# Two row points at a time in a convolution by polynomial points: interpolation in pairs, the infinite row by columns in two images, copies placed behind evictions

## The chip, the cores and the metric

The kernel runs on one core of one Trainium2 chip. The metric is the device time in microseconds of one execution; the time of a kernel is the median over several runs. TensorE multiplies matrices, VectorE does elementwise work between tiles, ScalarE does copies and activations, GpSimd (POOL) fills and loads, and SyncE (SP) issues most DMA transfers. In the profile these are PE, DVE, ACT, POOL and SP; PEld is the loading of weights into TensorE, which overlaps its matmuls.

## The reference, cut to what matters

The input x is 4 images of 256 channels, 64 by 64, in float32. Layer 0 makes 49 attention weights for each pixel and applies them to 49 shifted copies of the image; layer 1 whitens the result.

```
k = conv(x, w1, 7x7, dilation 2, padding 6) + b1        # 256 -> 128 channels
k = conv(k, w2, 1x1) + b2                               # 128 -> 49 channels
attn = softmax(k, axis=1)
y = sum over (u, v) of attn[:, 7u+v] * shift(x, 2u-6, 2v-6)
# layer 1, per group of 64 channels over all images and pixels:
Sigma = eps*I + cov(y);  five Newton steps P -> Sigma^(-1/2)
out = (P @ (y - mean(y))) * weight + bias
```

Nothing stands between the two convolutions, so the kernel folds w1 and w2 into one 7 by 7 convolution to 49 channels.

## The kernel before, in words

**Convolution by points.** A convolution with dilation 2 falls apart into four ordinary 7 by 7 convolutions, one for each parity of row and column. The kernel computes them as products of polynomials: along the rows and along the columns, input and filter are evaluated at seven points, numbered 0 to 6 in the code (the values 0, 1, -1, 2, -2, 1/2, and INF, the leading coefficient), multiplied, and interpolated. `row_eval` (L422) evaluates the input along the rows at one row point into the buffers `rb`, by VectorE. `col_eval` (L454) evaluates this along the columns, bank by bank, into the tiles `xh`. Column points go in three banks, `BANKS` = ((1, 2, 0), (3, 4, 6), (5,)), where 6 is INF. `weights` (L354) does the same for the filter; a row point's weights are computed once, stored in DRAM (`gd`), and loaded into `wr` by SP for each later image. There is one buffer for each `xh` and one `wr` for each bank, so the next row's operands can be made once the bank that reads them has been multiplied.

`conv_bank` (L483) multiplies one bank: a full row point takes 208 TensorE instructions over its three banks, in the kept order, and after each bank one ScalarE copy (L512, with high priority) evicts PSUM into the tile `pv` of the row. `col_interp` (L553) interpolates along the columns through `interpolate` (L517): 22 VectorE operations on 113 partitions, 19 of 162 elements and 3 of 144, and one ScalarE copy (L567) for the fourth output. Its results are row `br` of `zz`. When all row points of an image are there, `row_interp` (L570) does the same along the rows, 17 operations in its part 0 and 5 in its part 1, of 576 and 512 elements, and ScalarE adds the bias into the logits. The elementwise helpers are `add`, `sub` and `madd` (L300, L303, L307).

**The row point INF** does not go through column points. `direct_inf` (L632) loads its filter taps into `wi` and `direct` (L597, matmuls at L608) convolves the fourth row phase of the input along the columns directly: 56 TensorE instructions. The result goes to one of two tiles `zi`, whose last row POOL clears (L586).

**Order of the work.** Image 0 has a prologue in strict order: row points 1, 2 and 3 by columns, INF, 0, 4 and 5 directly (`direct0`), while the filter is being made. Then the loop at L1143 goes over images 1 to 3. In each, the list of steps is INF (cost 12) and for each of the rows 0 to 5 the three banks (costs 6, 5, 2). In image 1 INF comes after row 0, between the two parts of image 0's softmax (`soft`); in images 2 and 3 it is the first step. Each step, `conv_step` (L656), multiplies a bank, then prepares the same bank of the next row (`prepare`, L647), and after the last bank interpolates the columns. For the last two rows of an image this is held in written order (`in_order`) together with the parts of `row_interp`.

After each eighth of the summed costs, `gap` runs a piece of the weighted sum of the image before: transposes of the input (L926) copied to `xb` (L934), matmuls with `band` (L955), transposes of the result (L987) copied to `yt` (L995), and second moments (L1008). The attention weights go through DRAM (`sd`) into `band`, and VectorE transposes them there (L908). Softmax starts from transposed logits (L797) with a maximum on VectorE (L803, L806) and exponentials on ScalarE (L811).

[...] On VectorE and ScalarE a scheduler decides the order when the kernel is built, from dependences and priorities[...]. The last part of the kernel, after the last image's logits, finishes the weighted sum, computes the whitening matrices and writes the output.

Of the kernel before, what the change touches and what calls it, by code (L numbers as in the profile page):

```python
# [23 lines left out]
INF = 6  # L24
# [3 lines left out]
ROWS = (0, 1, 2, 3, 4, 5)  # L28
# [3 lines left out]
def kernel(  # L32
# [222 lines left out]
    zz = apool.tile([P, NP - 1, Q9, W], F32, name="zz")  # L255
    zi = [apool.tile([P, Q9, W], F32, name=f"zi{k}") for k in range(2)]
    for k in range(2):
        nc.gpsimd.memset(zi[k], 0.0)
    ct = apool.tile([P, Q8 * 4 * Q8, 4], F32, name="ct")
    it = ct.rearrange("p a b -> p (a b)")[:, :PT].rearrange("p (q b) -> p q b", q=Q9)  # L260
# [10 lines left out]
    gd = [dram.tile([P, nsl, NSK], F32, name=f"gd{b}") for b in range(NP - 1)]  # L271
# [41 lines left out]
    kept = {br: dram.tile([P, KS * NSK], F32, name=f"g{br}d") for br in (4, 5)}  # L313

# [40 lines left out]
    def weights(b, br, i):  # L355
# [9 lines left out]
        wt = apool.tile([P, ns, NSK], F32, tag=f"wr{i}", name=f"wr_{b}_{br}_{i}")  # L365
# [5 lines left out]
        if br == 0:  # L371
            g = [gr0[:, v] for v in range(KS)]
        elif br in kept:

            f = rb[0].rearrange("p q r c w -> p (q r c w)")[:, : KS * NSK]
            if i == 0:
                nc.sync.dma_start(f, kept[br])
            f = f.rearrange("p (v a r k) -> p v a r k", v=KS, a=NCC, r=2)
            g = [f[:, v] for v in range(KS)]
        else:  # L380
            g = [gbr[:, v] for v in range(KS)]
        g = [t.rearrange("p a r k -> p (a r k)") for t in g]
        e, o, e1 = (
            ct.rearrange("p a b -> p (a b)")[:, k * NSK : (k + 1) * NSK] for k in range(3)
# [38 lines left out]
    def row_eval(b, br, rb=rb):  # L423

        for pr in range(2):
            xs = slots[2 * b + pr].rearrange("p c (q a) w -> p a q c w", a=4)
            r = [t[:, :, pr] for t in rb]
            if br == 1:
                add(r[0], xs[:, 0], xs[:, 2])
                add(r[1], xs[:, 1], xs[:, 3])  # L430
            elif br == 0:
                nc.scalar.copy(r[2], xs[:, 0])
            for cc in range(NCC):
# [18 lines left out]
        return rb[{1: 2, 2: 0, 3: 0, 4: 1, 5: 2, 0: 2}[br]]  # L452
# [27 lines left out]
    pvs = {}  # L480

    def conv_bank(b, br, i, w):

        if i == 0:
            pvs[b, br] = apool.tile(
                [P, NP, Q9, 2 * Q9], F32, tag="pv", name=f"pv_{b}_{br}", bufs=2
            )
# [23 lines left out]
        with tc.high_priority():  # L511
            nc.scalar.copy(  # L512
                pvs[b, br][:K2, i0 : i0 + len(pts)].rearrange("p n q b -> p (n q b)"),
                cv[:K2, : len(pts)].rearrange("p n q b two -> p (n q b two)"),
            )

    def interpolate(pt, tmp, outs, cut, part=None):  # L517
# [9 lines left out]
        if part != 1:  # L527
# [14 lines left out]
            add(tmp, tmp, s4)  # L542
            madd(outs[0], lo(s1), 1.0 / 6, hi(c0))
            add(outs[2], lo(c6), hi(s3))
        if part != 0:
            madd(hh, tmp, -1.0 / 9, hh)
# [3 lines left out]
            madd(outs[1], lo(s4), 1.0 / 15, hi(s2))  # L550

    def phases(t):

        return [t[:, :, bass.ds(4 + a - R if a < R else 0, Q8, 4)] for a in range(4)]

    def col_interp(b, br, part=None):
        pv = pvs[b, br]
        pt = {c: pv[:K2, i] for i, c in enumerate(ORDER)}
        outs = phases(zz[:K2, br].rearrange("p q (w two) -> p q w two", two=2))
        cut = lambda t, k: t[:, :, 2 * k : 2 * (k + Q8)].rearrange("p q (b two) -> p q b two", two=2)  # L560
        t = it
        if part is not None:

            t = pvs[b, ROWS[-2]][:, 0]
        interpolate(pt, t[:K2], outs, cut, part)
        if part != 0:
            nc.scalar.copy(outs[3], cut(pt[5], 0))  # L567

    def row_interp(b, part):

        pt = {k: zz[:K2, k] for k in range(NP - 1)}
        pt[INF] = zi[b % 2][:K2]
# [4 lines left out]
        outs = [t[:, 0] for t in phases(lg[:K2].unsqueeze(1))]  # L577
        cut = lambda t, k: t[:, k : k + Q8]

        tr = zi[(b + 1) % 2]  # L580
        if part == 0:
            interpolate(pt, tr[:K2], outs, cut, 0)
            done_ = ((0, outs[0]), (2, outs[2]))
        else:
            interpolate(pt, tr[:K2], outs, cut, 1)
            nc.gpsimd.memset(tr[:, Q8], 0.0)  # L586
# [7 lines left out]
    def direct(b, br, s, ps, w, xr=None):  # L594
# [22 lines left out]
        z = zi[b % 2][:K2] if br == INF else zz[:K2, br]  # L617
# [7 lines left out]
    gi = dram.tile([P, KS, NCC * KT], F32, name="gi")  # L625
    nc.sync.dma_start(gi, tap[:, UPOS[3]].rearrange("p v a k -> p v (a k)"))

# [3 lines left out]

    def direct_inf(b):  # L632

        t = apool.tile([P, KS, NCC, KT], F32, tag="wi", name=f"wi_{b}")
        nc.sync.dma_start(t.rearrange("p v a k -> p (v a k)"), gi.rearrange("p v k -> p (v k)"))
        w = [t[:, v] for v in range(KS)]
        direct(b, INF, 0, conv_psum(), w)
# [5 lines left out]
    rows += [(b, br) for b in range(1, B) for br in ROWS]  # L643
# [11 lines left out]
    def conv_step(k, i):  # L655
# [14 lines left out]
        if i == len(BANKS) - 1 and not end:  # L670
            if b > 0 and br == ROWS[-2]:
                with in_order():
                    col_interp(b, br)
                    row_interp(b, 0)
            else:
                col_interp(b, br)

# [4 lines left out]
    def direct0(br, sr):  # L682
        if br in kept:
# [36 lines left out]
    nxt.update(weights(0, 3, 0))  # L720
    col_eval(xr, 0)
    direct0(0, 1)
    nxt.update(weights(0, 3, 1))
    col_eval(xr, 1)
    nxt.update(weights(0, 3, 2))
# [3 lines left out]
    col_interp(0, 1)  # L729
    col_eval(xr, 2)  # L730
    bank(2, 0)
    bank(2, 1)
    direct0(4, 0)
    bank(2, 2)
# [12 lines left out]
    col_interp(0, 2)  # L747
    direct0(4, 1)
    col_interp(0, 3)
    row_interp(0, 0)  # L750
    direct0(5, 0)
    for i in three:
        prepare(NR0, i)
    direct0(5, 1)
    row_interp(0, 1)
    strict[0] = False
# [386 lines left out]
    for b in range(1, B):  # L1143

        steps = []
        for r in range(len(ROWS)):
# [237 lines left out]
```

## Time and profile before

| quantity | value |
| --- | --- |
| median of 3 runs | 761.76 us (760.7 to 762.47) |
| the profiled execution | 767.08 us |
| its span in the profile | 765.3 us |
| TensorE busy | 710.7 us (93%) |
| VectorE busy | 630.3 us (82%) |
| ScalarE busy | 332.4 us (43%) |
| POOL busy | 34.4 us (4%) |
| granted TensorE clock, mean | 0.978 |
| convolution by points on TensorE (L502) | 253.7 us in 4368 instructions |
| direct row INF of images 1 to 3, with `wi` (L608) | 34.8 us in 168 instructions |

Durations come from one profiled execution, which took 5.3 us longer than the median of the runs. A line of the timeline gives the start, the busy time, the engine, the line of the code, the operation, output and inputs, the shape, and in brackets how long the engine was idle before and what ended that wait. "128x512 f32" is partitions by elements. A line of busy time by stage gives the stretch of the span, the sum, the busy time of PE, PEld, DVE, ACT and POOL, the granted clock, the DMA share and GB/s.

### The profile page before, as it was taken

What the parts mean: (1) busy time and instruction counts of PE and PEld (TensorE: products, weight loads), DVE (VectorE), ACT (ScalarE), POOL (GpSimd) and SP (SyncE); (2) the same over time, 40 slices, a digit from 0 to 9 for tenths busy, and PEclk for the clock granted to TensorE, in tenths of its full rate; (3) what the DMA queues carried; (4) which work ended last, traced back from release to release, by engine and by line L of the source; (5) the groups of instructions that cost most, each with busy time, mean ns of one, the idle gap of its engine ahead of it and who ended that gap; (6) DMA issues with size and microseconds to landing.
All of it is one profiled execution on the core that took longest, in us unless ns stands there. A gap on an engine that the chain in (4) does not pass through costs nothing.

```text
span 765.3 us, 18542 instructions
## 1 busy us (share of the span) xinstructions
PE 710.7 (93%) x7512; PEld 538.0 (70%) x7512; DVE 630.3 (82%) x1312; ACT 332.4 (43%) x958; POOL 34.4 (4%) x48
## 2 busy tenths in 40 slices
PE   6989899969899999989999999999999889998996
PEld 1449564365798887779988967798898768885322
DVE  3769999999899999989996899699979775645565
ACT  2413241025555454366444443635435473322464
POOL 0410000020000010001000100000000000000000
PEclk9999999979999999999999999999999999999999
DMA  8991110042654393056734920533532233362487
GB/s 323 238 322 65 39 75 38 1 155 68 200 153 156 122 351 91 20 160 205 235 120 141 313 70 1 155 90 110 166 88 80 49 115 128 115 251 111 190 362 327
DMA packets 59773, 114.76 MB, mean 150 GB/s; under 512 B 22903, under 2 KB 42024, under 8 KB 58920
## 3 DMA queue, kind: packets, MB, share of 16 engines
q1 hardware_dynamic: 55992, 94.71, 37.5%
q0 software_dynamic: 3696, 18.88, 7.2%
q8 instruction: 59, 0.97, 0.5%
q14 instruction: 26, 0.21, 0.1%
HBM read 66.23 MB, written 47.33 MB: 148 GB/s over the span
## 4 chain that ended last, share of the span: by engine, by line
DVE 43%; PE 32%; ACT 5%; issue 5%; DMA 2%; SPq 0%; DVEq 0%; ACTq 0%
PE y L955 10%; PE cv L502 7%; DVE xh L307 5%; PE tp L1324 4%; DVE rb L307 3%; DVE pv L307 3%; DVE zz L307 3%; DVE ct L307 3%; DVE ct L300 3%; DVE band L908 3%; PE sig L1008 3%; PE tp L987 2%; PE tp L926 2%; DVE pv L303 2%; DVE rb L300 2%
## 5 line engine op out<-in xcount | busy, mean ns | idle before, releaser
L502 PE MATMUL cv<-xh,wr 128*49 128x128 f32 x4368 | 253.7, 278 | 14.3 <-DVE xh L300 11.5
L502 PEld LDWEIGHTS cv<-xh,wr 128*49 128x49 f32 x4368 | 247.3, 125 | 19.9 <-issue 12.9
L955 PE MATMUL y<-band,xb 128*128 128x224 f32 (+2 forms) x640 | 153.4, 379 | 12.5 <-ACT xb L934 8.3
L955 PEld LDWEIGHTS y<-band,xb 128*128 128x128 f32 x640 | 111.2, 196 | 34.4 <-ACT xb L934 10.8
L974 ACT ACTIVATE slot<-y,pivot 128x512 f32<-128x512 f32 x53 | 36.7, 740 | 60.0 <-PE y L955 60.0
L512 ACT COPY pv<-cv 113x486 f32<-113x486 f32 (+1 forms) x63 | 29.8, 474 | 74.9 <-PE cv L502 73.7
L995 ACT COPY yt<-tp 128x256 f32<-128x256 f32 x128 | 45.5, 379 | 34.8 <-PE tp L987 33.8
L926 PE MATMUL tp<-ident,slot 128*128 128x128 f32 x256 | 50.3, 299 | 7.1 <-ACT yt L995 7.1
L987 PE MATMUL tp<-ident,slot 128*128 128x128 f32 x256 | 52.0, 299 | 4.0 <-ACT xb L934 1.4
L908 DVE STREAM_TRANSPOSE band<-band 128x960 f32<-128x960 f32 (+1 forms) x48 | 50.8, 1059 | 4.9 <-DMA band<-sd 4.8
L987 PEld LDWEIGHTS tp<-ident,slot 128*128 128x128 f32 x256 | 41.3, 205 | 13.9 <-issue 4.5
L926 PEld LDWEIGHTS tp<-ident,slot 128*128 128x128 f32 x256 | 40.0, 206 | 14.4 <-ACT yt L995 9.0
L857 ACT COPY zt<-d 32x112 f32<-32x112 f32 (+2 forms) x156 | 45.0, 288 | 1.7
L811 ACT ACTIVATE d<-tp,mx 128x49 f32<-128x49 f32 x128 | 37.0, 336 | 15.1 <-DVE mx L806 15.1
L307 DVE SCALAR_TENSOR_TENSOR xh<-ct 128x512 f32<-128x512 f32 x42 | 27.7, 681 | 12.2 <-PE cv L502 12.0
L934 ACT COPY xb<-tp 128x256 f32<-128x256 f32 x87 | 30.4, 376 | 15.8 <-PE tp L926 15.2
L1008 PE MATMUL sig<-yt 128*64 128x65 f32 x1024 | 36.9, 225 | 0.0
L1008 PEld LDWEIGHTS sig<-yt 128*64 128x64 f32 x1024 | 32.5, 138 | 6.0 <-issue 4.4
L608 PE MATMUL cv<-slot,wi 128*49 128x496 f32 (+3 forms) x168 | 34.8, 571 | 0.0
L934 DVE COPY xb<-tp 128x256 f32<-128x256 f32 x41 | 16.4, 421 | 22.2 <-PE tp L926 22.2
L307 DVE SCALAR_TENSOR_TENSOR pv<-pv 113x162 f32<-113x162 f32 x105 | 33.5, 319 | 1.0
L419 ACT ACTIVATE wr<-wr 128x392 f32<-128x392 f32 (+1 forms) x36 | 17.3, 512 | 31.1 <-DVE wr L300 18.8
(224 smaller groups left out, 999.9 us busy)
## 6 DMA issues: line engine op xcount, KB each, us to landing
out_dram<-out SPq DMA_DIRECT2D x32, 512.0 KB, 3.4
sd<-zt SPq DMA_DIRECT2D x16, 896.0 KB, 3.9
slot<-in_x_dram POOLq DMA_DIRECT2D x12, 1024.0 KB, 9.6
band<-sd SPq DMA_DIRECT2D x128, 84.0 KB, 2.1
wr<-gd SPq DMA_DIRECT2D x15, 588.0 KB, 3.8
wr<-gd SPq DMA_DIRECT2D x15, 490.0 KB, 3.6
spill<-slot POOLq DMA_DIRECT2D x3, 2048.0 KB, 8.4
back<-spill SPq DMA_DIRECT2D x3, 2048.0 KB, 7.7
```

Source lines behind the costliest of these rows:

```text
L300: return in_turn(TT(o, a, b, ALU.add))
L307: return in_turn(STT(o, a, f, b, ALU.mult, ALU.add))
L502: nc.tensor.matmul(cv[h * HB : h * HB + KT, k, sr : sr + n, sc : sc + n], wv[:, sc, sr, cc], xh[bc][:, :n, h * NCC + cc, :n], start=(j == ...
L811: nc.scalar.activation(d[:, h, i], lt[i // NI][:, i % NI, h, :KT], AF.Exp, bias=mx[:, i, h : h + 1], accum_out=s[:, h, i : i + 1],)
L857: ins = nc.scalar.copy(o, i)
L908: nc.vector.transpose(f, f)
L926: nc.tensor.transpose(t[:, cc * P : (cc + 1) * P], xt[:, cc, CR * m : CR * (m + 1), bass.ds(pc, SW, 2)], ident,)
L934: (nc.vector.tensor_copy if tail else nc.scalar.copy)(xb, t[:, :C])
L955: nc.tensor.matmul(ps[:, cc, q0 - half * HALF : q1 - half * HALF, :], xb[:, cc * P : (cc + 1) * P], rhs, start=(k == 0), stop=(k == len(PI ...
L987: nc.tensor.transpose(t[:, cc * P : (cc + 1) * P], yt[:, cc, CR * i : CR * (i + 1), bass.ds(pc, SW, 2)], ident,)
L995: nc.scalar.copy(yb.rearrange("p a g c -> p (a g) c")[:, :, :GW], t[:, :C].rearrange("p (e c) -> p e c", c=GW),)
L1008: nc.tensor.matmul(sig[g * GW : (g + 1) * GW, cc], yb[:, cc, g, :GW], yb[:, cc, g], start=(count[0] == 0 and cc == 0), stop=(count[0] == 4 ...
```

## The change

1. **Pairs of rows.** `ROWS` gets INF in front, and `PAIRS` = ((INF, 0), (1, 2), (3, 4)) names rows that are interpolated along the columns together, once the second of them has been multiplied. The rotating `pv` tiles become one tile with three slots: the first of a pair takes slot 0 or 2 in turn, the second always slot 1. `col_interp` builds one access pattern over both slots. Outputs 0 and 1 stay one operation for each row (`each`). Row 5 stays alone, and so does row 0 of image 1. In image 0, rows 1 and 2 go together.
2. **INF through column points** in images 2 and 3, as the image's first row: its filter is half as wide (104 TensorE instructions for the row in each image, where a full row has 208), computed once in image 2 from taps loaded through `rb[0]`. Its `row_eval` is a ScalarE copy into `rb[1]`, its row in `zz` replaces the tiles `zi`. The INF row of image 1 stays direct and moves to the end of the prologue. `direct_inf` and `wi` go.
3. **Late copies.** In images 1 to 3, the ScalarE copy of the fourth output of all pairs but the last is created at the next row's bank 1 and tied behind that bank's eviction on ScalarE.
4. **Prologue.** Row 3's banks come before row 4's filter, the first pair is interpolated after `row_eval(0, 5)`, `direct0(5, 0)` comes before `col_interp(0, 3)`, and the preparation of image 1's first row is split around `direct0(5, 1)`, `row_interp(0, 1)` and the INF row of image 1.
5. **Steps and gaps.** The costs of a half-wide row are halved (3, 2.5, 1), so the gaps stand at other places among the steps: in images 2 and 3 the first comes after bank 0 of row 0.

```diff
-ROWS = (0, 1, 2, 3, 4, 5)
+ROWS = (INF, 0, 1, 2, 3, 4, 5)
+PAIRS = ((INF, 0), (1, 2), (3, 4))
+AT = {br: k for k, br in enumerate(ROWS)}
...
-    zz = apool.tile([P, NP - 1, Q9, W], F32, name="zz")
-    zi = [apool.tile([P, Q9, W], F32, name=f"zi{k}") for k in range(2)]
+    zz = apool.tile([P, NP, Q9, W], F32, name="zz")
+    NV = 3
+    pv = apool.tile([P, NV, NP, Q9, 2 * Q9], F32, name="pv")
...
+    kept[INF] = dram.tile([P, KS * NSK // 2], F32, name="gi")
+    nc.sync.dma_start(kept[INF], tap[:, UPOS[3]].rearrange("p v a k -> p (v a k)"))
...
+            elif br == INF:
+                nc.scalar.copy(r[1], xs[:, 3])
...
+            if any(br == p[1] and (b, p[0]) in slot for p in PAIRS):
+                slot[b, br] = 1
+            else:
+                slot[b, br] = 2 * (groups[0] % 2)
+                groups[0] += 1
...
         with tc.high_priority():
-            nc.scalar.copy(
-                pvs[b, br][:K2, i0 : i0 + len(pts)].rearrange("p n q b -> p (n q b)"),
+            last = nc.scalar.copy(
+                pv[:K2, slot[b, br], i0 : i0 + len(pts)].rearrange("p n q b -> p (n q b)"),
                 cv[:K2, : len(pts)].rearrange("p n q b two -> p (n q b two)"),
             )
+        if i == 1:
+            while later:
+                tc.add_manual_dep(
+                    later.pop()().ins, last.ins.name,
+                    mybir.DependencyInfo(
+                        mybir.DependencyClass.NoSync, mybir.DependencyReason.DATA),
+                    reason="later",
+                )
...
-            madd(outs[0], lo(s1), 1.0 / 6, hi(c0))
+            for o, x, y in each(outs[0], lo(s1), hi(c0)):
+                madd(o, x, 1.0 / 6, y)
             add(outs[2], lo(c6), hi(s3))
+            add(s3, tmp, s4)
...
     def col_interp(b, br, part=None):
+        brs = br if isinstance(br, tuple) else (br,)
+        s0, ds = slot[b, brs[0]], slot[b, brs[-1]] - slot[b, brs[0]]
+        v = pv[:K2, s0]
+        v = bass.AP(
+            tensor=v.tensor,
+            offset=v.offset,
+            ap=[list(v.ap[0]), [PT, NP], [ds * NP * PT, len(brs)], [2 * Q9, Q9], [1, 2 * Q9]],
+        )
...
+        def end():
+            ins = nc.scalar.copy(outs[3], cut(pt[5], 0))
+            if INF in brs:
+                nc.gpsimd.memset(zz[:, AT[INF], Q8], 0.0)
+            return ins
+        if part is None and br != PAIRS[-1] and b > 0:
+            later.append(end)
+        elif part != 0:
+            end()
...
-    rows += [(b, br) for b in range(1, B) for br in ROWS]
+    rows += [(b, br) for b in range(1, B) for br in ROWS[1 if b == 1 else 0 :]]
...
     row_interp(0, 1)
+    direct(1, INF, 0, acc[:, 0], [tap[:, UPOS[3], v] for v in range(KS)])
+    prepare(NR0, 1)
+    prepare(NR0, 2)
...
-        for r in range(len(ROWS)):
-            k = NR0 + len(ROWS) * (b - 1) + r
-            for i, cost in enumerate((6, 5, 2)):
-                steps.append((cost, lambda k=k, i=i: conv_step(k, i)))
-        inf = (12, lambda b=b: direct_inf(b))
+        for k, (bk, br) in enumerate(rows):
+            if bk == b:
+                for i, cost in enumerate((6, 5, 2)):
+                    steps.append(
+                        (cost * len(taps(br)) / 2, lambda k=k, i=i: conv_step(k, i))
+                    )
         if b == 1:
-            steps[:3] = [
-                *steps[:3], (0, lambda: soft(0, 0)), inf, (0, lambda: soft(0, 1)),
-            ]
-        else:
-            steps.insert(0, inf)
+            steps.insert(0, (0, lambda: soft(0, 0)))
+            steps.insert(4, (0, lambda: soft(0, 1)))
```

## The prediction

> **What bounds the kernel now.** I read the page's header and busy times first, then the chain that ended last, then busy time by stage, and last the timelines of TensorE and VectorE around the places where one waits for the other.
>
> ```profile
> span 765.3 us, 18542 instructions
> PE 710.7 (93%) x7512; PEld 538.0 (70%) x7512; DVE 630.3 (82%) x1312; ACT 332.4 (43%) x958; POOL 34.4 (4%) x48
> ...
> DVE 43%; PE 32%; ACT 5%; issue 5%; DMA 2%; SPq 0%; DVEq 0%; ACTq 0%
> ```
>
> TensorE is busy 93%, yet the chain that ended last runs longer over VectorE (43%) than over TensorE (32%). Two engines share the bound, in different stretches. Busy time by stage tells which where (columns after start:end: sum, then PE, PEld, DVE, ACT, POOL busy, granted clock, DMA share, GB/s). The stages are mine: prologue with image 0, image 1 and the boundary to image 2, middle of image 2, boundary to image 3, image 3.
>
> ```profile
> 28.70:176.00 147.30, 132.88 (x1227) 81.01 (x1227) 135.51 (x260) 37.66 (x79) 18.68 (x21) 0.95 0.32 104
> 176.00:343.60 167.60, 159.11 (x1868) 130.54 (x1867) 159.59 (x346) 87.99 (x291) 6.34 (x6) 0.98 0.46 148
> 343.60:425.00 81.40, 79.78 (x1145) 74.06 (x1146) 69.21 (x143) 40.52 (x131) 3.93 (x3) 1.00 0.57 190
> 425.00:475.00 50.00, 48.22 (x502) 36.83 (x499) 48.62 (x89) 20.92 (x44) 3.52 (x3) 1.00 0.39 114
> 475.00:620.00 145.00, 136.91 (x1798) 124.31 (x1792) 125.04 (x279) 72.73 (x254) 0.99 (x6) 0.99 0.35 104
> ```
>
> VectorE is full in 176–344 (159.6 of 167.6) and 425–475 (48.6 of 50); only the middle of an image leaves it 14 to 15% free. TensorE is nearly full in the same two stretches: what covers a VectorE crunch there is TensorE work that needs nothing from VectorE. Its timeline names it:
>
> ```profile
> 157.53 7.43 PE L502 MATMUL cv<-xh,wr 128*49 128x128 f32 x96 [5.58 <-DVE xh L300]
> 167.72 8.12 PE L502 MATMUL cv<-xh,wr 128*49 128x128 f32 x112 [2.76 <-DVE zz L300]
> 300.81 11.59 PE L608 MATMUL cv<-slot,wi 128*49 128x512 f32 x56
> 453.45 11.59 PE L608 MATMUL cv<-slot,wi 128*49 128x512 f32 x56
> ```
>
> The last two are the direct convolution of row point INF at each image boundary: 11.59 us that read only the input slot. The first two show 8.3 us (5.58 + 2.76) in which TensorE waits for VectorE at the end of the prologue. Prices come from VectorE's timeline:
>
> ```profile
> 126.84 0.33 DVE L303 TENSOR_TENSOR pv<-pv 113x162 f32<-113x162 f32 x1
> 127.20 0.33 DVE L300 TENSOR_TENSOR pv<-pv 113x162 f32<-113x162 f32 x1
> ...
> 312.87 0.76 DVE L307 SCALAR_TENSOR_TENSOR zz<-zz 113x576 f32<-113x576 f32 x1
> ...
> 322.08 1.03 DVE L803 TENSOR_REDUCE mx<-tp 128x8 f32<-128x392 f32 x2
> ```
>
> 162 elements take 0.33 us and 576 take 0.76: (0.76 - 0.33)/414 = 1.04 ns an element, plus a fixed part. From start to start dependent operations stand 0.36 us apart (126.84 to 127.20); in this timeline independent ones of that size stand 0.24 to 0.25 apart.
>
> [...] The trace gives 0.245 - 162/960 = about 0.075 us where independent and 0.19 where dependent, so a pair saves more where nothing stands between its steps. [...] the late copy (zz L567) waits for pv L307 17 times, 50.4 us in all and 7.1 at the longest, on ScalarE.
>
> **The change part by part.**
>
> Row pairs. One `col_interp` alone runs from 126.49 to 133.28: 6.79 us, 19 operations of 162 and 3 of 144. A pair has 19 of 324: 19 x 162/960 = 3.2 us more; outs[2] of 288, 0.15 more; outs[0] and outs[1] once more each, 2 x 0.22. Together 10.6 us against 13.6 for two: -3.0 alone, about -1.6 where independent work already fills the gaps. Seven pairs replace two singles (images 0 to 3: 1, 2, 2, 2): -11 to -21, and -16.8 if four run alone and three filled. A pair (INF,0) where a single stood costs +3.8, twice. I assume that the hand-made stride costs nothing; bounds 0 to +0.15 us an operation (a second fixed part), or 0 to +3 us a pair.
>
> INF by columns, images 2 and 3. TensorE loses 112 direct instructions (2 x 11.59 = 23.2) and gains 208 convolutions of half a row (a full row of 208 runs 11.76, so 5.9 each, 11.8): -11.4. VectorE gains `col_eval` per image: two of 1024 at 1.13 from start to start and seven of 512 at 0.66, 6.9; and once, in image 2, 20 weight operations of 98 elements at 0.1 + 0.11, 4.2. ScalarE gains per image two row copies at 1.05, two of 512 at 0.68, and three evictions for two: about 5.5. Summed over the kernel, VectorE gains 2 x (6.9 + 3.8) + 4.2 = 25.6 and saves 16.8: near 639 instead of 630. The sign matters: the fuller engine of the crunches gets fuller, and the emptier one emptier. SP loads one weight half-row more and no `wi`; POOL loses four waits (zi L586, 212 us in all, nothing urgent behind) and gets memsets of one row; I put both at 0, at most +1.
>
> INF of image 1. It moves ahead of the first softmax. 8.3 of its 11.6 us fill the idle shown above, and the first pair takes 3 us off the prologue's VectorE. The first mx comes about 9 us sooner (178 to 169).
>
> Image 1 to its boundary. VectorE is full from 178 on, so of those 9 only 2.3 are left when (1,1)'s inputs are ready; pairs (1,2) and (3,4) bring `row_interp(1,0)` to end near 291.8 instead of 299. Then 4.2 of weights and 6.9 of INF inputs are inserted and part of the next row's evaluation (9.1 us of 1024- and 2048-element adds, about two thirds of it) comes ahead of the softmax in the changed program's order, which the build gives: INF's first inputs at 296, the next two banks at 311 and 316, mx at about 332.6 against 323. TensorE formerly had the 11.59 us at 300.8 to do meanwhile; now it has 2 us of bank I.0 and waits for I.1. Against mx 9.6 later stand 5.5 us of conv (2,0) already done and 1 to 2 of band work: **+2.4** by 352.
>
> Middle of image 2: TensorE-bound, **0 to -1**.
>
> Boundary 2 to 3: the same once more without the weights. Before, VectorE runs without a gap from 425.17 to 475 with TensorE covered by the 11.59 us at 453.45. It now gets +6.9 and a pair (1.6 to 3 saved), while TensorE, 5.7 us lighter, idles 4.6 and 5.4 at banks I.1 and I.2: **+4.7** by 509.
>
> Image 3 and tail: the pair (3,4) lets the logits come later than the single row 4 did: **+1 to +2**. Late copies: those 50 us of waiting no longer stand before evictions, but TensorE's waits on ScalarE after 343 come to about 6 us, with other copies in them: **0 to -3**, I take -1.5. The tail from the last moments on is the same.
>
> Sum: 2.4 - 0.5 + 4.7 + 1.5 - 1.5 = 6.6, rounded up to 7 for copies queued behind row copies. 767.1 (the profiled execution) + 7 = 774. The profiled execution is 5.3 above the median of the runs (761.76), so the median becomes about **768.8**.
>
> **Rivals.**
> A, faster, 0.16: TensorE is the bound everywhere. For it speak 93% and -11.4 us of its work, the 8.3 us filled, and VectorE's 14% free in the middles. Its place is the two boundaries: if I.1 and I.2 are ready when TensorE comes to them, losses there vanish and 761.8 - 8 = about 754 results. It decides from 7 us less of VectorE work ahead of I.1 at each boundary. Against it: 48.6 of 50 us.
> B, slower still, 0.20: a queue stall. INF's row copy on ScalarE waits for a slot that is reloaded one bank (about 5 us) later than the copy would like, and copies to yt and xb stand behind it; or a band transpose, placed earlier on VectorE, waits for its DMA (band L908 waited 4.8 us in all before). Each 2 to 6 us on a full engine: 772 to 779.
> C, no gain, 0.16: prologue's gain and boundaries' loss cancel: 758 to 765, about 762. What speaks for it: the 8.3 us are certain, the loss is spread over covers I could only estimate.
> Mine: 0.48, 765 to 773.
>
> **How the numbers follow.** A measurement of this kernel can hardly tell less than 0.2% (1.5 us). A gives faster 0.16; C gives faster 0.05, same 0.06, slower 0.05; B and mine slower 0.68, of which I hand 0.01 to same. Faster 0.21, same 0.07, slower 0.72. The range takes B's upper and half of A: 755 to 779; its own range for the likeliest is 765 to 773. The pair's stride at its upper bound (+3 x 9 pairs, about a third on the path) would add 9 and lies at the top end.
>
> **What would show it.** Right: VectorE near 639 busy with about 98 fewer instructions; 324-element operations at 0.49 us; TensorE near 699; its two waits at the prologue's end gone; at the boundaries waits of 4 to 10 us of matmuls on xh L300 and L307 ahead of INF's banks; a larger share of VectorE in the chain. Wrong: boundary waits under 3 us (A), waits of band transposes on DMA or of rb copies on a slot (B), a 324-element operation over 0.6 us.

## The result and the profile after

The changed kernel takes 780.62 us (778.72 to 783.51, 4 runs) against 761.74 us before (760.7 to 762.47, 4 runs): ratio 1.0252, 95% interval 1.0211 to 1.0293. The forecast was 768.8 with a range of 755 to 779. The direction was forecast, and so were long waits at both boundaries; the loss, 18.9 us, is more than twice the 7.0 that were forecast.

The page of the changed kernel: header, busy times and the chain by engine.

```profile
span 776.9 us, 18669 instructions
PE 699.8 (90%) x7608; PEld 539.7 (69%) x7608; DVE 642.6 (83%) x1214; ACT 343.2 (44%) x971; POOL 33.7 (4%) x45
...
PE 52%; DVE 26%; ACT 4%; DMA 3%; issue 3%; SPq 1%; DVEq 0%; ACTq 0%
```

The work moved as forecast: TensorE 699.8 us (699 expected), VectorE 642.6 (639), 98 instructions fewer on VectorE. But TensorE now lies idle for 77 us of its span instead of 55. Busy time by stage tells where (start:end, sum, then PE, PEld, DVE, ACT, POOL busy, granted clock, DMA share, GB/s). The stretches hold about the same work as those shown before, later in time.

```profile
28.70:176.00 147.30, 142.39 (x1310) 79.45 (x1312) 141.98 (x255) 46.73 (x124) 19.75 (x20) 0.99 0.32 106
176.00:365.00 189.00, 157.54 (x2088) 144.09 (x2085) 178.93 (x352) 92.55 (x288) 4.67 (x5) 0.93 0.47 150
365.00:445.00 80.00, 79.03 (x1089) 72.86 (x1090) 60.44 (x102) 41.20 (x112) 7.31 (x5) 1.00 0.60 195
445.00:495.00 50.00, 37.71 (x442) 33.97 (x440) 48.69 (x75) 17.55 (x38) 0.00 (x0) 0.83 0.21 58
495.00:640.00 145.00, 135.74 (x1730) 122.32 (x1727) 123.10 (x244) 77.62 (x281) 0.99 (x6) 0.99 0.34 104
```

TensorE is idle for 31 us in image 1 with its boundary and 12 us at the boundary to image 3, VectorE stays full there, and the granted clock drops to 0.93 and 0.83 (0.98 and 1.00 before). The timeline of TensorE names the waits:

```profile
174.70 13.05 PE L520 MATMUL cv<-xh,wr 128*49 128x128 f32 x208 [2.35 <-ACT pv L530]
197.94 7.10 PE L520 MATMUL cv<-xh,wr 128*49 128x128 f32 x96 [10.19 <-DVE xh L306]
...
310.75 3.97 PE L520 MATMUL cv<-xh,wr 128*49 128x128 f32 x40 [10.24 <-ACT lgx L641]
315.92 6.42 PE L520 MATMUL cv<-xh,wr 128*49 128x128 f32 x112 [1.20 <-ACT xh L485]
...
468.36 4.62 PE L520 MATMUL cv<-xh,wr 128*49 128x128 f32 x40 [7.16 <-DVE xh L313]
476.85 8.46 PE L520 MATMUL cv<-xh,wr 128*49 128x128 f32 x112 [3.86 <-issue]
```

The last four are INF's banks 1 and, with row 0's bank 0 behind it, 2: 22.5 us of waiting at the two boundaries. The first two are in image 1: the 8.3 us of waiting at the prologue's end are gone, as forecast, and 12.5 us stand here instead.

**The two traces can't be subtracted as they are.** In the profiled execution of the kernel before, VectorE waits at the very start for the last piece of image 0's load. VectorE of the kernel before, then of the changed kernel, evaluating row point 1:

```profile
38.08 2.35 DVE L300 TENSOR_TENSOR rb<-slot 128x1024 f32<-128x1024 f32 x2
46.91 2.36 DVE L300 TENSOR_TENSOR rb<-slot 128x1024 f32<-128x1024 f32 x2 [6.47 <-DMA slot<-in_x_dram]
```

```profile
38.19 4.62 DVE L306 TENSOR_TENSOR rb<-slot 128x1024 f32<-128x1024 f32 x4
```

Without that wait the spans are 758.8 and 776.9 us, 18.1 apart, which is what the runs say (18.9). The experiments below follow this up.

### The profile page after: what moved, and what is told of

The parts are those of the page before. It is cut to its first block, busy times and chain, and to the rows that moved or that the text cites. A ratio compares the mean times of both kernels' runs of the same rounds, so it can differ in the third digit from the quotient of the medians.

```text
span 776.9 us, 18669 instructions
## 1 busy us (share of the span) xinstructions
PE 699.8 (90%) x7608; PEld 539.7 (69%) x7608; DVE 642.6 (83%) x1214; ACT 343.2 (44%) x971; POOL 33.7 (4%) x45
## 4 chain that ended last, share of the span: by engine, by line
PE 52%; DVE 26%; ACT 4%; DMA 3%; issue 3%; SPq 1%; DVEq 0%; ACTq 0%
PE cv L520 18%; PE y L998 13%; PE tp L1030 4%; PE tp L1364 4%; PE tp L969 3%; PE sig L1051 3%; DVE ct L313 3%; PE acc L659 3%; DVE xh L313 2%; DVE pv L313 2%; DVE band L951 2%; DVE zz L313 2%; DVE pv L309 2%; DMA band<-sd 2%; DVE ct L306 2%
## 5 line engine op out<-in xcount | busy, mean ns | idle before, releaser
L520 PE MATMUL cv<-xh,wr 128*49 128x128 f32 (+1 forms) x4576 | 270.1, 280 | 37.1 <-DVE xh L306 11.0
L520 PEld LDWEIGHTS cv<-xh,wr 128*49 128x49 f32 x4576 | 261.6, 126 | 43.3 <-issue 26.8
L998 PE MATMUL y<-band,xb 128*128 128x224 f32 (+2 forms) x640 | 151.5, 375 | 12.4 <-ACT xb L977 10.0
L998 PEld LDWEIGHTS y<-band,xb 128*128 128x128 f32 x640 | 109.6, 193 | 33.5 <-ACT xb L977 12.6
L530 ACT COPY pv<-cv 113x486 f32<-113x486 f32 (+1 forms) x69 | 33.1, 479 | 118.6 <-PE cv L520 118.4
L951 DVE STREAM_TRANSPOSE band<-band 128x960 f32<-128x960 f32 (+1 forms) x48 | 50.8, 1059 | 10.4 <-DMA band<-sd 10.3
L1030 PEld LDWEIGHTS tp<-ident,slot 128*128 128x128 f32 x256 | 41.4, 205 | 14.4 <-issue 4.5
L854 ACT ACTIVATE d<-tp,mx 128x49 f32<-128x49 f32 x128 | 37.2, 328 | 20.2 <-DVE mx L849 15.6
L313 DVE SCALAR_TENSOR_TENSOR xh<-ct 128x512 f32<-128x512 f32 x46 | 30.2, 684 | 14.9 <-PE cv L520 14.5
L313 DVE SCALAR_TENSOR_TENSOR pv<-pv 113x324 f32<-113x324 f32 (+1 forms) x84 | 35.9, 428 | 1.4
L659 PE MATMUL acc<-slot,tap 128*49 128x496 f32 (+3 forms) x168 | 34.6, 569 | 0.0
L306 DVE TENSOR_TENSOR ct<-rb 128x1024 f32<-128x1024 f32 (+2 forms) x32 | 30.5, 967 | 1.8 <-DMA rb<-g5d 1.2
```

The source lines that it names most:

```text
L306: return in_turn(TT(o, a, b, ALU.add))
L313: return in_turn(STT(o, a, f, b, ALU.mult, ALU.add))
L520: nc.tensor.matmul(cv[h * HB : h * HB + KT, k, sr : sr + n, sc : sc + n], wv[:, sc, sr, cc], xh[bc][:, :n, h * NCC + cc, :n], start=(j == ...
L659: nc.tensor.matmul(ps[h * HB : h * HB + KT, :, w0:w1_], w[v][:, cc], xs[:, :, cc, w0 + d : w1_ + d], start=(j == 0), stop=(j == len(order) ...
L951: nc.vector.transpose(f, f)
L998: nc.tensor.matmul(ps[:, cc, q0 - half * HALF : q1 - half * HALF, :], xb[:, cc * P : (cc + 1) * P], rhs, start=(k == 0), stop=(k == len(PI ...
```

## The experiments

My theory after the result was COVER: at the image boundaries the direct row INF was work that TensorE could do while VectorE was full, and the change took it away there and in image 1, and gave VectorE more to do. Its rivals were PAIRS (two rows at once hold back what TensorE needs) and QUEUE (ScalarE's ties and copies). Later runs added theories named in their expectations. Ratios are to the kernel before, on the same chip, with 95% intervals; differences between experiments are partly across chips, on all of which the kernel before took 761.4 to 761.7 us. "Held-back loads" is the edit of experiment 9. The edits are shown in part; `...` marks what is left out.

**1. INF direct again in images 2 and 3.**

```diff
-PAIRS = ((INF, 0), (1, 2), (3, 4))
+PAIRS = ((1, 2), (3, 4))
...
-    rows += [(b, br) for b in range(1, B) for br in ROWS[1 if b == 1 else 0 :]]
+    rows += [(b, br) for b in range(1, B) for br in ROWS[1:]]
...
+        if b > 1:
+            steps.insert(0, (12, lambda b=b: direct_inf(b)))
```

`direct_inf` does what it did before, with its taps in the third product slot; row 0 of images 2 and 3 is then interpolated alone.

> Changed kernel, but INF of images 2 and 3 direct again as first step of each image (cost 12; its taps are loaded into the third product slot, free at that moment). Pairs (1,2) and (3,4), late copies and INF of image 1 in the prologue stay. Theory COVER (the boundaries lost the direct row's cover and VectorE got fuller there): the waits of 10.2 + 1.2 us and 7.2 + 3.9 us on the INF banks go, VectorE loses about 25 us of work, 763 to 769 us (against 780.6 for the changed kernel). Rival PAIRS (interpolating two rows at once delays zz and holds xh back): stays at 777 or above. Rival QUEUE (ScalarE's ties and copies): above 775.

Measured: 763.26 us, ratio 1.0042 (1.0020 to 1.0063). INF by columns costs 17.4 us (780.62 - 763.26). I compared the start of the same matmul of the weighted sum in both traces, since they come in the same order (counted from 0): number 60 of 640 starts at 255.6 here and 255.7 in the changed kernel, number 240 (behind the first boundary) at 429.0 and 437.0, number 360 (behind the second) at 550.2 and 566.7, number 620 at 682.2 and 698.8. So all of it is made at the two boundaries, 8.0 and 8.5 us. There TensorE has the direct row again:

```profile
302.29 11.59 PE L659 MATMUL cv<-slot,pv 128*49 128x512 f32 x56
449.09 11.59 PE L659 MATMUL cv<-slot,pv 128*49 128x512 f32 x56
```

This puts the loss on INF by columns and not on the other pairs or the ties. It doesn't split the loss: the edit gives TensorE its cover back and also takes 21.2 us of work from VectorE (621.4 us busy instead of 642.6).

**2. No pairs.**

```diff
-PAIRS = ((INF, 0), (1, 2), (3, 4))
+PAIRS = ()
...
-        if part is None and br != PAIRS[-1] and b > 0:
+        if part is None and br != ROWS[-2] and b > 0:
...
-    col_interp(0, (1, 2))
+    col_interp(0, 1)
+    col_interp(0, 2)
```

In this kernel rows 1 and 3 of image 0 share a product slot, so row 1 of that image is interpolated from row 3's products and the output is not the reference's; the amount of work is the same. The late copies are tied for all rows but row 4.

> Changed kernel with every row interpolated alone (no pairs); INF by columns in images 2 and 3, late copies, prologue order stay. COVER: VectorE gets 14 to 20 us more work, half of it on the path at the boundaries and in image 1: 785 to 793 us. PAIRS: 765 to 774. QUEUE: within 2 us of 780.6.

Measured: 789.25 us, ratio 1.0380 (1.0326 to 1.0434), with VectorE 657.5 us busy instead of 642.6. Pairs gain 8.6 us in the changed kernel. PAIRS falls.

**3. INF of image 1 back in image 1.**

```diff
-    direct(1, INF, 0, acc[:, 0], [tap[:, UPOS[3], v] for v in range(KS)])
...
+            steps.insert(4, (12, lambda: direct_inf(1)))
```

> Changed kernel with INF of image 1 moved back from the prologue to behind row 0's banks in image 1, before the second half of the softmax. COVER: the wait of 10.2 us on the inputs of row 1 (at 197.9) is filled, but the waits of 5.6 and 2.8 us at the prologue's end come back: 776 to 782 us. If the move itself was what lost the time, 768 to 773.

Measured: 789.84 us, ratio 1.0375 (1.0349 to 1.0401): 9.2 us slower than the changed kernel, outside both expectations.

**4. Both INF edits undone.** The edits of 1 and 3 together. The first half of image 0's softmax stays ahead of row 0, where the change put it.

> Both INF edits undone: INF direct in all three images at its old places; pairs (1,2), (3,4), late copies and the new prologue order stay. COVER: VectorE loses some 12 us against the kernel before, half of it on the path: 752 to 760 us, faster than before (761.7). PAIRS: 765 or above.

Measured: 759.07 us, ratio 0.9979 (0.9961 to 0.9997). Against experiment 1, moving INF of image 1 into the prologue costs 4.2 us; in experiment 3, beside INF by columns, the same move gained 9.2. The two INF edits are not additive. In experiment 3 TensorE also waits 4.57 us for `xb` at 280.3, where ScalarE stands 5.68 us before the copies of INF's taps (their DMA is late) with the copies to `xb` behind them; the changed kernel has waits for `xb` too, of 2.10 and 3.09 us. More stands at the first boundary, where TensorE of experiment 3 waits already for INF's bank 0, and the changed kernel doesn't:

```profile
304.73 5.37 PE L520 MATMUL cv<-xh,wr 128*49 128x128 f32 x48 [5.62 <-DVE xh L306]
```

The wait and the slow matmuls (5.37 us instead of 2.87) are 8.1 us. Why bank 0 is late there stays open.

**5. The kernel before, profiled once more.** No edit.

> The kernel before, unchanged, profiled once more. Its first profiled execution took 767.1 us where its other runs lie at 757.9 to 763.4. If that trace holds a delay of its own, this one takes 759 to 764 us and some stretch of it is 4 to 6 us shorter; if profiling costs 5 us in this kernel, it takes 766 to 768 again.

Measured: 769.59 us, with a wait of 7.62 us at 48.04 for the same load as above. Both traces of the kernel before hold this wait; its other runs in that comparison lie at 759.6 to 763.8 us.

**6. TensorE kept busy through the waits, too much of it.**

```diff
+            pe(nc.tensor.matmul(ps[h * HB : h * HB + KT, :P], ident[:, :KT], ident,
+                                start=True, stop=True, skip_group_check=True))
...
+            steps.insert(1, (0, lambda b=b: fill((0, 0, 170, 130)[b])))
+            steps.insert(3, (0, lambda b=b: fill((0, 0, 20, 64)[b])))
```

> Changed kernel, with matrix products that nothing reads put into TensorE's queue where it waits at the two image boundaries: 170 and 130 small ones between banks 0 and 1 of INF (images 2 and 3), 20 and 64 between banks 1 and 2. The work to be done stays. Theory CLOCK (a wait also costs about 2 us of slower matmuls after it, as the 40 after the waits took 4.0 and 4.6 us instead of 2.3, and 112 took 8.5 instead of 6.5): 774 to 778 us. If the slow matmuls are not on the path, 779 to 783.

Measured: 799.67 us, ratio 1.0476 (1.0420 to 1.0532). Inconclusive: each of these products is two instructions (340 and 260 for 170 and 130), so they took 18.7 and 14.4 us, twice the waits. Its trace also had a load wait of 9.4 us. Experiment 10 repeats it.

**7. The first gap early.**

```diff
-                        (cost * len(taps(br)) / 2, lambda k=k, i=i: conv_step(k, i))
+                        (cost if len(taps(br)) == 2 else (12, 0, 0)[i],
+                         lambda k=k, i=i: conv_step(k, i))
```

> Changed kernel with the first gap of images 2 and 3 right behind INF's bank 0 instead of behind row 0's bank 0 (cost 12, 0, 0 for the three half banks), so that the piece of the weighted sum stands where TensorE waits. COVER (what is missing at the boundary is work for TensorE that needs nothing new from VectorE): the piece takes 6 to 8 us, so 768 to 775 us. If VectorE's work alone sets the boundary's length: 778 to 783.

Measured: 782.26 us (778.65 to 789.17), ratio 1.0277 (1.0209 to 1.0345), with a load wait of 11.65 us in the trace. Too noisy to tell; experiment 11 repeats it.

**8. INF's taps copied by GpSimd.**

```diff
+            cp = nc.gpsimd.tensor_copy if br == INF else nc.scalar.copy
-            nc.scalar.copy(o0[0], g0[0])
-            nc.scalar.copy(o1[0], g1[0])
+            cp(o0[0], g0[0])
+            cp(o1[0], g1[0])
...
```

> Changed kernel with the three copies of INF's taps (98 elements each, once, in image 2) on GpSimd instead of ScalarE. Theory TAPS (ScalarE waits 4.0 us for the taps' load, with copies to xb behind it, and TensorE waits 3.1 us for xb at 281.4): 3 to 5 us less, 775.5 to 778. If VectorE is behind anyway, 779.5 to 782.

Measured: 783.25 us, ratio 1.0283 (1.0248 to 1.0318), no gain. The wait of ScalarE for the taps is in the changed kernel's trace (3.95 us, before 280.62), but not what sets the boundary. TAPS falls.

**9. The loads of image 1 held back**, in the changed kernel and in the kernel before.

```diff
     for s in range(2, 4):
+        nc.gpsimd.tensor_copy(
+            store[s][:, :, 0, 0:1],
+            rb[2].rearrange("p q r c w -> p (q r c w)")[:, :NCC].unsqueeze(2),
+        )
         load_x(s, s, nc.gpsimd)
```

> Changed kernel with the loads of image 1 (slots 2 and 3, on GpSimd's queue) held back until VectorE has evaluated row point 1 of image 0, so that they can't run beside the last pieces of image 0's load. Theory LOAD (in some executions VectorE waits for image 0's last piece near 38 us: 6.5 and 7.6 us in the two traces of the kernel before, 0 in the changed kernel's, 11.7 and 9.4 in two experiments): the wait is gone in the trace, the spread of the times shrinks, 777 to 780 us. If image 1's load is needed early, it gets slower than 782.

> Kernel before with the same held-back loads. LOAD: the wait of 6.5 to 7.6 us is gone in the trace, whose execution then takes 760 to 762 us instead of 767 and 769; the median of all runs hardly moves (758 to 762), so that the two kernels with this edit stand 17 to 20 us apart, in the traces too.

Measured: the changed kernel 782.96 us (1.0284, 1.0253 to 1.0316), the kernel before 761.45 (1.0002, 0.9988 to 1.0015). VectorE of the kernel before with this edit:

```profile
38.15 4.62 DVE L300 TENSOR_TENSOR rb<-slot 128x1024 f32<-128x1024 f32 x4
```

The wait is gone and its profiled execution takes 760.19 us instead of 767 and 769. The issues in the traces show what goes with the delay. In the kernel before, with its wait of 6.47 us, SP issues the last load of image 0 at 34.59, after GpSimd's first load of image 1 at 33.99; in the changed kernel, without a wait, SP's last is at 33.45 and GpSimd's first at 33.66. The ten traces without held-back loads agree: where GpSimd's first issue leads SP's last by 0.1 us or less there is no wait, at 0.33 and 0.39 us it is 1.05 and 0.90 (experiments 1 and 2), and at 0.60, 0.73, 0.86 and 1.23 us it is 6.47, 7.62, 9.43 and 11.65 (the kernel before twice, experiments 6 and 7). With GpSimd's loads held back the wait is gone in both kernels. The median doesn't move, and the changed kernel's spread didn't shrink (779.8 to 785.2), so in the runs without a profile the wait was seldom or small. The use of this edit is in the traces: against this one of the kernel before (span 758.4), the changed kernel's trace can be read directly.

**10. TensorE kept busy, fitted to the waits.** As 6, with (80, 58) and (10, 30) products, and held-back loads.

> Changed kernel with held-back loads and, at the two boundaries, matrix products that nothing reads where TensorE waits, now fitted to the waits (8.8 and 1.1 us in image 2, 6.4 and 3.3 in image 3). CLOCK (slow matmuls after a wait are on the path): 4 to 6 us below the run with held-back loads alone, 773 to 776. If they are not, within 1.5 us of it. COVER alone says the latter.

Measured: 778.60 us, ratio 1.0228 (1.0200 to 1.0256), 4.4 us below the changed kernel with held-back loads. TensorE at the first boundary, first without the fill, then with it (L681 are the products that nothing reads):

```profile
300.49 2.87 PE L520 MATMUL cv<-xh,wr 128*49 128x128 f32 x48
312.08 4.62 PE L520 MATMUL cv<-xh,wr 128*49 128x128 f32 x40 [8.72 <-ACT lgx L641]
```

```profile
301.84 8.90 PE L681 MATMUL cv<-ident 128*49 128x128 f32 x160
310.72 2.48 PE L520 MATMUL cv<-xh,wr 128*49 128x128 f32 x40
...
475.89 8.06 PE L520 MATMUL cv<-xh,wr 128*49 128x128 f32 x112 [2.68 <-DVE xh L313]
```

The same 40 matmuls take 4.62 us behind a wait and 2.48 behind work. The mean granted clock rises from 0.961 to 0.978. Over 299 to 320 it is 0.76 without the fill and 1.00 with it. The intervals of the two ratios just touch (1.0253 to 1.0316 and 1.0200 to 1.0256), but the traces leave little doubt about CLOCK: work that nothing needs makes the kernel faster, and one wait of 2.68 us that was left open has a slow bank behind it again.

**11. The first gap early, with held-back loads.**

> Changed kernel with held-back loads and the first gap of images 2 and 3 directly behind INF's bank 0. COVER: TensorE does 6 to 8 us of the weighted sum while it would wait, once for each boundary, part of it given back by VectorE's order: 4 to 8 us below the run with held-back loads alone, 770 to 775. If VectorE alone sets the boundary's length, within 1.5 us of it.

Measured: 777.29 us, ratio 1.0199 (1.0169 to 1.0230), 5.7 below the changed kernel with held-back loads. This fits COVER: a third of the boundaries' 17 us comes back when the gap's work stands in the wait. It doesn't all come back, since the wait moves on:

```profile
312.23 1.21 PE L844 MATMUL tp<-ident,lgx 113*128 113x113 f32 x8 [1.18 <-ACT lgx L641]
...
323.11 13.36 PE L520 MATMUL cv<-xh,wr 128*49 128x128 f32 x192 [7.25 <-ACT wr L429]
```

INF's bank 1 finds its inputs, and bank 2 waits 7.25 us for the weights. Their copy stands on ScalarE behind the exponentials of the softmax, which the gap takes forward with it (its first maximum starts at 313.00 instead of 332.77). So the edit moves work of VectorE and ScalarE too, and 5.7 us is the sum of both.

**12. The rest of the change without the INF edits.** Four kernels, all with held-back loads and INF direct at its old places, but for the last of the four, which is the changed kernel.

> Pairs, late copies and new prologue order with INF direct at its old places (as in the run with both INF edits undone), and held-back loads. LOAD: as that run, 757 to 760 us, no wait for the load in its trace.

> The same, with the late copies not tied: each goes where the scheduler puts it, as in the kernel before. QUEUE (the tie moves waits of ScalarE away from evictions): 2 to 4 us slower, 760 to 763. If TensorE's waits for ScalarE had other causes: within 1 us.

> As the first of these, but only rows 1 and 2 are paired; row 3 is interpolated as soon as it is multiplied and row 4 alone, in every image. Theory SPIKE (the pair (3,4) puts 3.8 us of VectorE work into the boundary, and delays the last image's logits, where the pairs' lead of 4 us over the kernel before is lost): 753 to 757 us. If saved VectorE work counts wherever it is: 759 to 763.

> Changed kernel with held-back loads and rows 3 and 4 interpolated alone; the other pairs and both INF edits stay. SPIKE: 4 to 9 us less than the changed kernel with held-back loads (783.0), 774 to 779. If saved work counts wherever it is: 783 to 788.

The edits besides the held-back loads:

Late copies not tied:

```diff
-        if part is None and br != PAIRS[-1] and b > 0:
+        if False:
```

Rows 3 and 4 alone:

```diff
-PAIRS = ((1, 2), (3, 4))
+PAIRS = ((1, 2),)
...
-        if part is None and br != PAIRS[-1] and b > 0:
+        if part is None and br != ROWS[-2] and b > 0:
...
+            if b > 0 and br in (3, 4):
+                with in_order() if br == 4 else nullcontext():
+                    col_interp(b, br)
+                    if br == 4:
+                        row_interp(b, 0)
```

The second hunk also ties the late copy of row 3; with the pair, rows 3 and 4 share one copy and it isn't tied.

| kernel | median us | ratio to before |
| --- | --- | --- |
| pairs (1,2) and (3,4), copies tied | 758.50 | 0.9972 (0.9953 to 0.9991) |
| the same, copies not tied | 765.36 | 1.0053 (1.0036 to 1.0069) |
| pair (1,2) only, copies tied | 755.81 | 0.9930 (0.9909 to 0.9951) |
| changed kernel, rows 3 and 4 alone | 783.16 | 1.0284 (1.0222 to 1.0346) |

The tie is worth 6.9 us, more than expected. Against the tied kernel, the untied one falls back in image 3: number 340 of the weighted sum is level (526.3 and 526.2), number 380 is 4.0 later. There ScalarE of the untied kernel, then TensorE:

```profile
529.39 0.45 ACT L613 COPY zz<-pv 113x288 f32<-113x288 f32 x1 [2.45 <-DVE pv L313]
```

```profile
530.99 4.70 PE L1007 MATMUL y<-band,xb 128*128 128x320 f32 x12 [2.63 <-ACT xb L986]
```

The late copy waits 2.45 us for VectorE, the copy to `xb` stands behind it on ScalarE and starts at 530.56, TensorE waits 2.63 us, and the 12 matmuls then take 4.70 us instead of 3.18. So a wait of 2.63 us is worth 4.15, with the slower matmuls behind it; the rest of the 6.9 wasn't traced to places.

Pairing (3,4) costs 2.7 us in these kernels. SPIKE named the boundary and the last image's logits. Here are the transposes of that image's first softmax (L849, after the edit L854), with the pair and without:

```profile
598.54 1.48 PE L849 MATMUL tp<-ident,lgx 113*128 113x113 f32 x8 [2.19 <-ACT lgx L641]
```

```profile
594.60 1.18 PE L854 MATMUL tp<-ident,lgx 113*128 113x113 f32 x8
```

They come 3.9 us earlier without the pair, but 3.5 of it is there at number 240 (419.5 instead of 423.0) and still at number 340 (522.7 instead of 526.2): most of the gain is made in image 1 and its boundary. At number 620 it is 4.6, so about 1 us can belong to the last image.

In the changed kernel the same unpairing does nothing (783.16 against 782.96): what the pair costs shows only in the kernels with INF direct.

**13. The last pair taken away.** As "pair (1,2) only", without pairs in images 1 to 3.

```diff
-            if b > 0 and br in (3, 4):
+            if b > 0 and br in (1, 2, 3, 4):
...
```

> As the run with only rows 1 and 2 paired (755.8 us), with no pair left in images 1 to 3: what remains against the kernel before is the new prologue order, image 0's pair, the tied late copies and held-back loads. If the pair (1,2), 4.6 us of VectorE's time in three images, stands in the middle of the images, where VectorE has slack: within 1.5 us of 755.8. If saved VectorE work counts there too: 758 to 761.

Measured: 758.40 us, ratio 0.9950 (0.9933 to 0.9966). The intervals overlap with those of one pair (0.9909 to 0.9951), so whether the pair (1,2) gains anything is not settled; the prologue order, image 0's pair, the tied copies and the held-back loads are together faster than before without it.

The version with pair (1,2), tied copies, the new prologue order, INF direct at its old places and held-back loads beats both kernels: 755.81 us, 0.7% below before (0.5 to 0.9%).

## Why the prediction was wrong

It had the sign and the boundaries, and was 11.8 us too low. Against the kernel before with held-back loads, whose trace has no load wait, the starts of the same matmuls of the weighted sum give the sum term by term. The gaps stand at other places among the steps now (part 5 of the change): at number 60 the changed kernel has 80 matmuls of the convolution more behind it, at number 160 it has 32 more. At 11.80 us for 208 that is 4.5 and 1.8 us of work, which the fifth column takes off. At the other three numbers the same rows and banks are done in both.

| number of 640, place | before, held-back loads | changed | later by | the same, for equal work | the forecast's sum there |
| --- | --- | --- | --- | --- | --- |
| 60, in image 1 | 251.1 | 255.7 | 4.6 | 0.1 | about -2.3 |
| 160, behind the first boundary | 349.1 | 361.4 | 12.3 | 10.5 | +2.4 |
| 240, middle of image 2 | 425.5 | 437.0 | 11.5 | 11.5 | +1.9 |
| 360, behind the second boundary | 549.4 | 566.7 | 17.3 | 17.3 | +6.6 |
| 620, near the end | 678.6 | 698.8 | 20.2 | 20.2 | +6.6 |

So most of what is missing was lost between image 1 and the first boundary: 11.5 us at number 240, where the forecast had 1.9.

**The step that failed: the lead in image 1.** The forecast let the pairs "bring `row_interp(1,0)` to end near 291.8 instead of 299", a lead of 7.2 us, and set it against what the boundary costs. Here are the last write of that part into the logits and VectorE from the first maximum of image 0's softmax to that write's end, in the kernel before with held-back loads and then in the changed kernel:

```profile
292.13 0.68 DVE L300 TENSOR_TENSOR lgx<-zi,zz 113x512 f32<-113x512 f32 x1
170.71:292.81 122.10, 115.06 (x1458) 98.62 (x1457) 117.88 (x266) 65.77 (x214) 5.63 (x4) 1.00 0.53 172
```

```profile
290.72 0.68 DVE L306 TENSOR_TENSOR lgx<-zz 113x512 f32<-113x512 f32 x1
161.87:291.40 129.53, 110.91 (x1534) 103.39 (x1531) 121.54 (x231) 65.49 (x212) 7.16 (x9) 0.95 0.49 160
```

The first maximum does come 8.8 us sooner (161.87 instead of 170.71), as forecast. But the stretch behind it takes 129.5 us instead of 122.1, so 1.4 us of lead are left and not 7.2. VectorE has 3.7 us more to do there (121.5 instead of 117.9), among it evaluations that stood ahead of the first maximum and now stand behind it (four additions of 1024 elements into `rb` instead of one), and it is idle for 8.0 us instead of 4.2. No run takes the two apart. Its longest wait there is this:

```profile
186.66 1.18 DVE L951 STREAM_TRANSPOSE band<-band 128x960 f32<-128x960 f32 x1 [3.38 <-DMA band<-sd]
```

This is rival B's band transpose, placed ahead of its transfer's end; in all, such waits took 10.3 us instead of 4.8. The interpolation of the row before stands behind this transpose on VectorE and continues at 187.76. At the boundary the first maximum of the softmax is then 16.1 us later (331.44 instead of 315.30), where 9.6 were forecast.

That the forecast's positions were met closely in the changed kernel's own trace (INF's bank 1 at 311 forecast and 310.75 measured, bank 2 at 316 and 315.92, the maximum at 332.6 and 331.44) is luck. They were built on a trace in which everything behind 47 us stood 6.47 us later because of the load wait, and the changed kernel's execution didn't have that wait. I did see that the execution was 5.3 us above its median and subtracted this as a constant at the end. The question "where in the trace are these 5 us" had a one-line answer in VectorE's timeline.

**The boundaries' price.** It was forecast as 4.7 us each, after everything that was set against it; experiment 1 puts it at 17.4 in all. The waits themselves were nearly right: at the second boundary 10.0 us forecast (4.6 + 5.4) and 11.0 measured. A term for slow matmuls behind them is missing. From experiment 1 to the changed kernel TensorE's idle time up to number 620 grows by 20.5 us, its work falls by the 11.4 us that were forecast, and number 620 stands 16.6 later, which leaves 7.5 us. Of these, 5.7 stand behind the boundaries' waits (40 matmuls in 3.97 and 4.62 us instead of 2.48 twice, 112 in 8.46 instead of 6.42). Experiment 10 wins back 4.4.

**INF of image 1 (the step "8.3 of its 11.6 us fill the idle shown above").** It did fill that idle. With INF at its old place, experiment 4's trace has a wait of 7.60 us at the prologue's end and 208 slow matmuls behind it (14.18 us instead of 11.80); with INF moved, experiment 1's has none there and 2.36 and 10.65 us in image 1 instead. So the waiting moved on and didn't go, and I priced the waits that the row filled and not the cover that it left. What the move is worth in the changed kernel can't be told from this: it costs 4.2 us with INF direct in images 2 and 3 (experiment 1 against 4) and gains 9.2 beside INF by columns (experiment 3).

**Row pairs.** Right in price: the 324-element operations took 0.486 us on the mean (0.49 forecast). Those of 162 took 0.320, and 162 elements more at 1.04 ns (the forecast's 162/960) make 0.49 by estimate, so the hand-made stride shows no cost. In effect they are worth 8.6 us in the changed kernel (experiment 2).

**Boundary 2 to 3, image 3.** +4.7 forecast, 5.8 measured. The end was put at +1.5 and, with the late copies, 0; 2.9 came, and about as much in experiment 4's trace over the same stretch (3.0), so it doesn't come from INF by columns. That the tie is worth 6.9 us with INF direct (experiment 12) where I took 1.5 doesn't explain this, it makes it larger; what the tie gains beside INF by columns wasn't measured.

**Rivals.** A fell by the 22.5 us of waits. B came nearest in time (772 to 779), but of its two mechanisms only the transposes showed; the copies of row INF on ScalarE didn't wait for a slot (two waited 4.4 us in all for VectorE), and the late taps that did wait were not on the path (experiment 8). The chain did not show it right: I expected a larger share of VectorE, and it fell from 43 to 26%.

## What to carry to other kernels

Work that an engine can do without news from the bound engine can be worth more than its busy time where it stands, whatever the totals say: here TensorE had 11.4 us less to do, and the kernel took 17.4 us longer. Before moving or shrinking such work, find the next wait that it covers. A lead that is won early on the bound engine need not arrive where it is needed: of 8.8 us, 1.4 were left. Price a new wait of TensorE with the slower matmuls behind it (40 took 4.62 us instead of 2.48 here). And when a profiled execution is slower than its runs, find the one place before using its positions as a baseline; here a wait of 6.47 us for a load at the start had shifted everything behind it.

## What the runs showed of the hardware

**A wait cost more than its length.** Behind waits of 7 to 10 us, 40 matmuls took 4.0 to 4.6 us instead of 2.5 (4.62 / 2.48 = 1.9); behind 3.86 us, 112 took 8.46 instead of 6.42. In the changed kernel these matmuls start at 310.75, 468.36 and 476.85, and the granted clock is 0.50 from 303.64 to 313.88 and from 464.07 to 481.13.

Waits of 2.35, 2.63 and 2.68 us were also followed by slow matmuls (208 in 13.05 us instead of 11.80, 12 in 4.70 instead of 3.18, 112 in 8.06 instead of 6.42), but not every wait of that length was: behind one of 2.36 us in experiment 1, 208 matmuls took 11.80. In the changed kernel the wait of 2.35 us lasts from 172.35 to 174.70, and the granted clock is 1.00 in the 3.41 us up to 173.94 and 0.50 from there to 177.35. What makes one wait of this length slow and another not was not shown.

**The order of two loads issued about 1 us apart**, on SP's and GpSimd's queues, went with a wait of VectorE for image 0's last piece of up to 11.65 us. GpSimd's first issue led SP's last by 0.60 to 1.23 us where the wait was 6.47 to 11.65, and by 0.1 us or less, or not at all, where there was none; with GpSimd's loads held back the four traces of experiments 9 to 11 don't have the wait.
